# Fifth block product of Q in a two-level Winograd projection: quarter sums accumulated in PSUM onto ScalarE copies, interleaved with the seventh block product

## The chip, the cores and the metric

The kernel runs on one core of a Trainium2 chip. The metric is device time in microseconds (us) of the whole program; lower is better. TensorE (PE in the profile) multiplies, with its weight loads listed apart as PEld; VectorE is DVE, ScalarE is ACT, GpSimd is POOL, and SyncE (SP) issues the transfers.

## The reference

Two layers of the same form are applied to `x` of shape (8, 512, 32, 32), all in float32. Cut to what matters here, one layer is

```python
xn = group_norm(x) * gn_scale + gn_bias              # per image; xt is (512 channels, 1024 positions)
qkv = einsum('oc,bcn->bon', qkv_w, xt) + qkv_b       # three 512x512 weights times 512x1024
q, k, v = split(qkv, 3)                              # 8 heads of 64
attn = softmax(einsum('bhdi,bhdj->bhij', q, k) / 8)
out = einsum('bhij,bhdj->bhdi', attn, v)
out = einsum('oc,bcn->bon', proj_w, out) + proj_b + x
```

Eight images and two layers make 16 units, worked one after the other.

## The kernel before, in words

**Order of a unit.** A unit first forms Q, then K, then V (the first unit: Q, V, K), then the output projection of the unit before it, and then runs attention over 64 steps. Everything is issued in an order written out by hand, on in-order engine queues; callbacks `done(g)` place DVE and POOL work of other kinds between the products. A recording layer adds the semaphore waits. PSUM is held in four tiles of two banks (128 x 2 x 512 float32): `sbank[0]` and `sbank[1]`, which appear as `s` in the profile, and `apair[0]` and `apair[1]`, which appear as `a`.

**Block products.** Each projection splits its operands 2 by 2 and forms seven block products (Winograd's form of Strassen's scheme) in `blocks` (L422), with P1 to P7 combined into four output blocks: C11 = P1 + P2, and with U2 = P1 + P6 and U3 = U2 + P7, C22 = U3 + P5, C21 = U3 + P4, C12 = U2 + P5 + P3. A plain block product for Q and K, `block_product` (L405), is four matmul calls of 128 x 512, two for each of two row halves; each call is two PE matmuls. The tile of products 1 and 2 is `bx` = `apair[0]`; of 6, 7 and 4 it is `by` = `sbank[0]`; of 5 and 3 it is `bz` = `apair[1]`. The order is 1, 6, 2, 7, 5, 4, 3. After 6, `summed` forms u2 from `by` on DVE; after 7 it forms u3 (two operations at L624), and product 4 then accumulates onto what 6 and 7 left in `by`.

**Inner products.** In 15 of the 16 units (all but the first) some block products are formed by seven quarter products of 128 x 256 again: 2, 5, 4 and 3 of Q; 1, 2, 7, 5, 4 and 3 of K; 2, 3 and 4 of the output projection. `inner_products` (L437) runs the quarter products in the order `ORDER` = 1, 2, 3, 6, 5, 4, 7 (for Q). Quarters 2, 3 and 4 go straight into three quarters of the block's own tile. Quarters 1, 6 and 7 are accumulated one after the other in one place, `one`, and 5 in another, `two`; after each of these four ACT copies that place to a fresh SBUF tile `rest` (L460), so that `rest` holds 1, 1+6, 1+6+7 and 5. POOL then adds two quarters of `rest` to others (`fold`, L466 to L469) and adds `rest` to the result (`rests`, L650, or L647 and L648 where a half has to be split). For Q's product 2, `one` is in `sbank[1]` and `two` in `apair[1]`; for its product 5, `one` is in `sbank[1]` and `two` in `apair[0]`; for 4, `apair[0]` and `sbank[1]`.

**What follows.** `c11` (L605) evacuates C11 of Q by two ACT operations between product 2 and product 7. `others` (L636, L637) forms C22, C21 and C12 on DVE. The right factors of the inner products come from four subtractions each: those of 2 and 5 on POOL before the unit starts (L1088), those of 4 and 3 on POOL in between (L578), those of K's 1 and 7 on DVE in between (L578 too). K's P1 is summed on DVE at L492 to L495 from `bx` and `rest`.

Of the kernel before, what the change touches and what calls it, by code (L numbers as in the profile page):

```python
# [18 lines left out]
P = 128  # L19
# [13 lines left out]
def fast_path(ctx, tc, x, qkv_wT, proj_wT, vecs, groups, out, flag):  # L33
# [15 lines left out]
    nc = tc.nc  # L49
# [4 lines left out]
    FD = 512  # L54
    NH = N // FD
    H = P // 2
    FD2 = FD // 2
# [6 lines left out]
    def pool(name, bufs, **kw):  # L64
        return ctx.enter_context(tc.tile_pool(name=name, bufs=bufs, **kw))
# [9 lines left out]
    tpool = pool("tpool", 1)  # L75
    tmppool = pool("tmppool", 1)
    trpool = pool("trpool", 2)
# [7 lines left out]
    sbank = [ps.tile([P, 2, FD], F32, tag=f"s{i}", name=f"s{i}") for i in range(2)]  # L85
# [316 lines left out]
    class Unit:  # L402
        pass

    def block_product(bank, a, b, tokens, start, stop, between=None):  # L405
        for i in range(4 if tokens else 2):
            if i == 1 and between is not None:
                between()
            if tokens:
                dst = bank[:, i // 2, (i % 2) * FD2 : (i % 2 + 1) * FD2]  # L410
            else:
                dst = bank[:, i, :]
            for c in range(2):
                at, moving = (b, a) if tokens else (a, b)

                nc.tensor.matmul(  # L416
                    dst, at[:, c, ts(i, P)], moving[:, c, :],
                    start=start and c == 0 and not (tokens and i % 2),
                    stop=stop and c == 1, skip_group_check=True,
                )  # L420

    def blocks(name, left, right, tokens, c11, others, done, u3_in, summed, inner={}, rests=None,  # L422
               u2_in=(trpool, "tr"), between=None, behind=None, p1=None):

        bx, by, bz = apair[0], sbank[0], apair[1]
        sums, taken = [], []

        def products(bank, k, start, stop, between=None):
            block_product(bank, left[k], right[k], tokens, start, stop, between)

        def inner_products(bank, k, first=False):  # L437

            if k not in inner:
                products(bank, k, first, k != 5)
                return None
            a, b, one, two, order, room = inner[k]
            one, two, rest = one[:, 0, :FD2], two[:, 0, :FD2], room(f"m{k}_{name}")
            dst = {
                1: one, 6: one, 7: one, 5: two,
                2: bank[:, 0, :FD2], 3: bank[:, 0, FD2:], 4: bank[:, 1, :FD2],
            }
            to = {  # L450
                1: rest[:, 0, :FD2], 6: rest[:, 0, FD2:], 7: rest[:, 1, :FD2], 5: rest[:, 1, FD2:]
            }

            def step(j):
                nc.tensor.matmul(  # L455
                    dst[j], a[j], b[j], start=j in (1, 5) or first and j in (2, 4),
                    stop=j not in (1, 6), skip_group_check=True,
                )
                if j in to:
                    taken.append(nc.scalar.copy(to[j], dst[j]))  # L460

            for j in order if k != 1 else order[:-1]:
                step(j)
            return (rest, partial(step, order[-1])) if k == 1 else rest

        def fold(rest):  # L466
            add = nc.gpsimd.tensor_add
            add(rest[:, 0, FD2:], rest[:, 0, FD2:], rest[:, 1, FD2:])  # L468
            add(rest[:, 1, FD2:], rest[:, 1, :FD2], rest[:, 1, FD2:])  # L469

        def add_rest(r, h, rest, alone=None):

            if rest is not None:
                fold(rest)
                rests(r, h, rest, alone)

        def work(pool, tag, k):
            sums.append(pool.tile([P, 2, FD], F32, tag=tag, name=f"{k}_{name}"))
            return sums[-1]

        fresh = p1 is not None or 1 in inner
        if p1 is not None:
            sums.append(p1)
            done(sums)
            products(by, 6, True, False)
        elif fresh:
            p1 = work(accpool, "acc", "p1")
            rest, last = inner_products(bx, 1, True)
            done(sums)
            products(by, 6, True, False, last)  # L490
            add = nc.vector.tensor_add
            add(rest[:, 0, FD2:], rest[:, 0, FD2:], rest[:, 1, FD2:])  # L492
            add(p1[:, 0, :], bx[:, 0, :], rest[:, 0, :])
            add(p1[:, 1, :FD2], bx[:, 1, :FD2], rest[:, 1, :FD2])
            add(p1[:, 1, FD2:], rest[:, 1, :FD2], rest[:, 1, FD2:])  # L495
        else:
            products(bx, 1, True, False, between)
            if behind is not None:
                behind()
            p1 = work(accpool, "acc", "p1")  # L500
            nc.scalar.copy(p1, bx)  # L501
            done(sums)
            products(by, 6, True, False)
        u2 = work(*u2_in, "u2")
        summed(0, u2, by, p1)
        done(sums)
        rest = inner_products(bx, 2, fresh)
        c11(bx, p1 if fresh else None, rest)
        add_rest(0, 0, rest)
        done(sums)  # L510
        seventh = inner_products(by, 7)
        u3 = work(*u3_in, "u3")
        summed(1, u3, by, p1)
        if seventh is not None:
            fold(seventh)
        done(sums)
        twice = inner_products(bz, 5, True)
        others(1, 1, bz, u3, twice)
        add_rest(1, 1, twice, u3)
        if seventh is not None:  # L520
            rests(1, 1, seventh)
        done(sums)
        rest = inner_products(by, 4)
        others(1, 0, by, p1)
        add_rest(1, 0, rest)
        if seventh is not None:
            rests(1, 0, seventh)
        done(sums)
        rest = inner_products(bz, 3)
        others(0, 1, bz, u2, twice)  # L530
        add_rest(0, 1, rest, u2 if twice is not None else None)
        if twice is not None:
            rests(0, 1, twice)
        done(sums)
        return taken[-1:]

# [3 lines left out]
    ORDER, ORDER_5, ORDER_1 = (1, 2, 3, 6, 5, 4, 7), (1, 5, 2, 6, 3, 4, 7), (2, 3, 1, 4, 5, 6, 7)  # L540

    def room_of(pool, tag):
        return lambda name: pool.tile([P, 2, FD], F32, tag=tag, name=name)

    def inner_of(w, sel, left):


        x, z, s1 = apair[0], apair[1], sbank[1]
        p = room_of(ppool, "p")
        plan = {  # L550
            "q": {
                2: (s1, z, ORDER, room_of(tpool, "o1")), 5: (s1, x, ORDER, room_of(tpool, "o2")),
                4: (x, s1, ORDER, room_of(tpool, "o4")), 3: (s1, x, ORDER, room_of(tpool, "o1")),
            },
            "k": {
                1: (s1, z, ORDER_1, lambda _: w.k[1].rearrange("p (a b) -> p a b", a=2)),
                2: (s1, z, ORDER, room_of(tmppool, "tmp")), 7: (z, s1, ORDER, room_of(tpool, "o4")),
                5: (s1, x, ORDER_5, p), 4: (x, s1, ORDER, p), 3: (s1, x, ORDER, p),
            },
        }[sel]  # L560
        return {
            k: (inner_lefts(k, left[k], w.made[sel][k]), w.inner[k], *plan[k]) for k in INNER[sel]
        }

    def projections(w, rest, between=None):
# [4 lines left out]
        l, _ = units[u]  # L570
# [25 lines left out]
        def pairs(sel, bias):  # L596
            tiles = getattr(w, sel)
# [44 lines left out]
            def rests(r, h, rest, alone=None):  # L642
                add = nc.gpsimd.tensor_add
                for i in range(2):
# [4 lines left out]
                    else:  # L649
                        w.last[sel].append(add(cols, cols, rest[:, i, :]))  # L650

            left, inner = w.lefts["qk".index(sel)], {}
            if w.inner:
                inner = inner_of(w, sel, left)
            blocks(
                f"{sel}_{u}", left, w.right, False, c11, others, done,
                (accpool, "acc") if w.inner else (ppool, "p"), summed, inner, rests, **early[sel],
            )

        def values():  # L660
# [372 lines left out]
    tiles = [xn[:, c, :] for c in range(CC)]  # L1033
# [7 lines left out]
    right, mixing = mix_right("x_0", xn[:, :2], xn[:, 2:])  # L1041
# [10 lines left out]
    between, mixing_w = norm_first(xn, first_weights, mixing)  # L1052
# [14 lines left out]
    for u in range(2 * B):  # L1067
        w = Unit()
# [4 lines left out]
        for sel in "qk":  # L1073
            tiles = [
                qkpool.tile([P, N], F32, tag=sel, name=f"{sel}_{u}_{pr}") for pr in range(CC)
            ]
            setattr(w, sel, tiles)
        if u > 0:
            w.made, w.inner, parts = old.made_next, {}, {}
            for k in INNER["q"]:  # L1080
                room = ppool.tile([P, 4, FD2], F32, tag="p", name=f"r{k}_{u}")
                w.inner[k], parts[k] = mix_inner(right[k], room, nc.gpsimd)

            for k, pr in ((1, 3), (7, 2)):
                room = w.k[pr].rearrange("p (a b) -> p a b", a=4)
# [35 lines left out]
        between = None  # L1121
# [3 lines left out]
        if u + 1 < 2 * B:  # L1125
            xn = load_xn(u + 1)
            nxt = norm_parts(u + 1, xn)
            right, mixing = mix_right(f"x_{u + 1}", xn[:, :2], xn[:, 2:])
# [357 lines left out]
```

## Time and profile before

| what | value |
|---|---|
| median of three runs | 3257.72 us |
| the three runs | 3256.99, 3257.72, 3259.81 us |
| span of the profiled execution | 3256.9 us (first to last instruction; no other time of that execution is given) |
| PE busy, share of the span | 3244.5 us, 100% |
| DVE, ACT, POOL busy | 2715.3, 1650.2, 1216.3 us |
| granted TensorE clock, mean | 0.999 |
| PE matmuls of plain block products, 128 x 512 | one every 0.43 us |
| PE matmuls of inner products, 128 x 256 | one every 0.216 us |

Matmuls are pipelined: the duration shown for one (0.59 us for 512 columns, 0.38 us for 256) is longer than the spacing of two. The profile covers one execution; its span lies 0.8 us under the median.

### The profile page before, as it was taken

The page shows a single profiled execution, that of the slowest core. Times are in us where ns is not written, and L with a number is a line of the kernel's source. Part 1 is how long each engine was busy: PE and PEld are TensorE (multiplying, and loading weights), DVE is VectorE, ACT ScalarE, POOL GpSimd, SP SyncE. Part 2 cuts the span into 40 slices and gives each one's busy share as a digit, 9 for nine tenths or more (in the row PEclk, how much of TensorE's full clock was granted, in tenths as well). Part 3 has the DMA queues.
Part 4 walks back from the last instruction along what each step waited for, and adds up shares of the span by engine and source line. Part 5 has one row for each costly group of instructions (what it writes and reads, how often), then busy time and mean ns, then how long its engine had stood idle before and what let it go on. Part 6 is the DMA issues. An engine that isn't in the chain of part 4 may idle for free.

```text
span 3256.9 us, 56805 instructions
## 1 busy us (share of the span) xinstructions
PE 3244.5 (100%) x22206; PEld 1863.3 (57%) x22206; DVE 2715.3 (83%) x3488; ACT 1650.2 (51%) x2296; POOL 1216.3 (37%) x1207
## 2 busy tenths in 40 slices
PE   9999999999999999999999999999999999999999
PEld 5465474654746547465574655747556474564743
DVE  5887978789787897989979889797897978979786
ACT  1653626546274463744637446373563735637354
POOL 2054171531706317063270732607126071350710
PEclk9999999999999999999999999999999999999999
DMA  3112120121201212023120121201212012120111
GB/s 104 48 45 79 46 79 28 45 79 46 85 22 45 85 43 86 18 71 114 55 87 27 45 86 46 85 16 45 86 46 85 17 54 76 46 85 22 67 71 48
DMA packets 86463, 192.51 MB, mean 59 GB/s; under 512 B 22960, under 2 KB 34992, under 8 KB 84272
## 3 DMA queue, kind: packets, MB, share of 16 engines
q1 hardware_dynamic: 86192, 188.82, 17.0%
q8 instruction: 180, 2.95, 0.4%
q14 instruction: 91, 0.75, 0.1%
HBM read 148.00 MB, written 39.19 MB: 57 GB/s over the span
## 4 chain that ended last, share of the span: by engine, by line
PE 96%; DVE 3%; issue 0%; DMA 0%; ACT 0%; SPq 0%; DVEq 0%
PE a L848 26%; PE s L820 25%; PE s L416 14%; PE a L416 12%; PE a L455 10%; PE s L455 9%; DVE acc L867 1%; PE a L820 1%; PE s L766 0%; PE a L766 0%; DVE tr L880 0%; PE s L361 0%; DVE acc L865 0%; DVE ao L874 0%; DMA xn<-x_dram 0%
## 5 line engine op out<-in xcount | busy, mean ns | idle before, releaser
L828 ACT ACTIVATE p<-s 128x1024 f32<-128x1024 f32 x976 | 998.0, 1024 | 558.0 <-PE s L820 516.6
L848 PE MATMUL a<-p,v 64*64 64x512 f32 x8192 | 1099.8, 589 | 0.0
L820 PE MATMUL s<-q,k 64*64 64x512 f32 x7808 | 1058.1, 590 | 0.0
L867 DVE TENSOR_TENSOR acc<-acc,p 128x1024 f32<-128x1024 f32 x768 | 968.6, 1261 | 61.7 <-ACT p L828 13.0
L848 PEld LDWEIGHTS a<-p,v 64*64 64x64 f32 x8192 | 383.2, 131 | 495.8 <-ACT p L828 350.2
L820 PEld LDWEIGHTS s<-q,k 64*64 64x64 f32 x7808 | 383.5, 133 | 431.9 <-issue 422.8
L1088 POOL TENSOR_TENSOR r<-xn 128x256 f32<-128x256 f32 x30 | 49.5, 1649 | 1175.7 <-DVE acc L867 1038.3
L650 POOL TENSOR_TENSOR k<-k,m_k 128x512 f32<-128x512 f32 x180 | 259.6, 1463 | 0.0
L865 DVE TENSOR_TENSOR acc<-p,p 128x1024 f32<-128x1024 f32 x128 | 156.2, 1220 | 20.5 <-ACT p L828 13.9
L312 POOL TENSOR_TENSOR y<-var,half 128x4 f32<-128x4 f32 (+1 forms) x17 | 33.2, 1950 | 344.4 <-DVE var L310 344.4
L880 DVE STREAM_TRANSPOSE tr<-acc 128x1024 f32<-128x1024 f32 x128 | 157.9, 1234 | 0.0
L650 POOL TENSOR_TENSOR q<-q,m_q 128x512 f32<-128x512 f32 x120 | 157.2, 1325 | 0.0
L890 DVE TENSOR_REDUCE red<-tr 128x32 f32<-128x1024 f32 x128 | 154.4, 1206 | 0.6
L538 DVE TENSOR_TENSOR u_v<-s,p_v 128x1024 f32<-128x1024 f32 x32 | 39.2, 1224 | 123.7 <-PE s L416 123.7
L501 ACT COPY p_o<-a 128x1024 f32<-128x1024 f32 x15 | 15.2, 1012 | 244.2 <-PE a L416 244.2
L874 DVE TENSOR_TENSOR ao<-a,tmp 128x512 f32<-128x512 f32 x128 | 88.0, 688 | 60.9 <-ACT tmp L873 59.6
L460 ACT COPY m_q<-s 128x256 f32<-128x256 f32 x150 | 55.9, 373 | 145.3 <-PE s L455 142.7
L468 POOL TENSOR_TENSOR m_o<-m_o 128x256 f32<-128x256 f32 x45 | 34.2, 760 | 251.7 <-ACT m_o L460 251.7
L416 PE MATMUL s<-x_t,s2w 128*128 128x512 f32 x256 | 117.5, 592 | 0.0
L416 PE MATMUL a<-w,xn 128*128 128x256 f32 x496 | 112.1, 379 | 0.0
L460 ACT COPY m_k<-s 128x256 f32<-128x256 f32 x165 | 61.5, 373 | 93.8 <-PE s L455 90.2
L334 ACT ACTIVATE xn<-xn,shift,scale 128x512 f32<-128x512 f32 x124 | 99.5, 804 | 10.9 <-DVE shift L330 10.9
(291 smaller groups left out, 5130.5 us busy)
## 6 DMA issues: line engine op xcount, KB each, us to landing
rb<-drec SPq DMA_DIRECT2D x128, 256.0 KB, 3.9
xn<-mid SPq DMA_DIRECT2D x36, 512.0 KB, 7.9
il<-ilk SPq DMA_DIRECT2D x15, 1152.0 KB, 7.0
xn<-x_dram SPq DMA_DIRECT2D x32, 512.0 KB, 7.0
x<-x_dram SPq DMA_DIRECT2D x32, 512.0 KB, 5.5
x<-mid SPq DMA_DIRECT2D x28, 512.0 KB, 4.9
il<-ilq SPq DMA_DIRECT2D x15, 768.0 KB, 4.2
mid<-u_o SPq DMA_DIRECT2D x32, 256.0 KB, 2.1
```

Source lines behind the costliest of these rows:

```text
L334: nc.scalar.activation(cols, cols, AF.Identity, bias=st["shift"][:, c - lo : c - lo + 1], scale=st["scale"][:, c - lo : c - lo + 1],)
L416: nc.tensor.matmul(dst, at[:, c, ts(i, P)], moving[:, c, :], start=start and c == 0 and not (tokens and i % 2), stop=stop and c == 1, skip ...
L455: nc.tensor.matmul(dst[j], a[j], b[j], start=j in (1, 5) or first and j in (2, 4), stop=j not in (1, 6), skip_group_check=True,)
L460: taken.append(nc.scalar.copy(to[j], dst[j]))
L650: w.last[sel].append(add(cols, cols, rest[:, i, :]))
L820: nc.tensor.matmul(bank[e * H : (e + 1) * H, j, :], w.k[pr][j * H : (j + 1) * H, t * P + e * H : t * P + (e + 1) * H], w.q[pr][j * H : (j ...
L828: exp = nc.scalar.activation(p, bank, AF.Exp, scale=SCALE)
L848: nc.tensor.matmul(banks[r][j * H : (j + 1) * H, :], w.v[rows, t, lo : lo + D], p[rows, j, :], start=(t == 0), stop=(t == NT - 1),)
L865: nc.vector.tensor_add(acc, state["first"], p)
L867: nc.vector.tensor_add(acc, acc, p)
L880: nc.vector.transpose(tr, state["acc"].pop(c))
L890: nc.vector.tensor_reduce(red[:, :, qh, :], state["tr"].rearrange("p j (f i) -> p j f i", i=BL), AX.X, ALU.add)
```

## The change

The change concerns Q's fifth block product in the 15 units with inner products. Its quarter sums are no longer all copied to SBUF. A new function `seeded` runs the quarters in the order 1, 6, 7, 5, 2, 3, 4. Quarter 1 is formed in `one`, and ACT copies it into the first quarter of `bz`; quarter 6 is accumulated onto it, and ACT copies 1+6 into the third quarter of `bz`; quarter 7 goes to `two`, and ACT copies it to an SBUF tile `late`; quarter 5 is accumulated onto 1+6, and ACT copies that into the second and the fourth quarter of `bz`. Quarters 2, 3 and 4 are then accumulated onto the copies. `one` and `two` are the two banks of `sbank[1]`. The four matmul calls of the seventh block product (a 0 in the sequence below) are issued in between, as `fillers`. `lates` adds `late` on POOL, by one operation for each of two output blocks. The second place of Q's product 2 moves from `apair[1]` to the second bank of `sbank[1]`. `fold` and `rests` of the fifth product are no longer called.

```diff
@@ block_product @@
+                step = partial(
+                    nc.tensor.matmul, dst, at[:, c, ts(i, P)], moving[:, c, :],
...
+                if steps is None:
+                    step()
+                else:
+                    steps.append(step)
@@ blocks @@
+        def seeded(bank, k, fillers, scratch, room):
+            a, b = inner[k][:2]
+            one, two = scratch[:, 0, :FD2], scratch[:, 1, :FD2]
+            late = room(f"m{k}_{name}")[:, 0, :FD2]
+            dst = {
+                1: one, 6: one, 5: one, 7: two,
+                2: bank[:, 0, :FD2], 3: bank[:, 0, FD2:], 4: bank[:, 1, :FD2],
+            }
+            seeds = {
+                1: [bank[:, 0, :FD2]], 6: [bank[:, 1, :FD2]], 5: [bank[:, 0, FD2:], bank[:, 1, FD2:]],
+                7: [late],
+            }
+            fillers = iter(fillers)
+            for j in (1, 0, 6, 7, 0, 5, 2, 0, 3, 0, 4):
+                if j == 0:
+                    next(fillers)()
+                    continue
+                nc.tensor.matmul(
+                    dst[j], a[j], b[j], start=j in (1, 7), stop=j not in (1, 6), skip_group_check=True
+                )
+                for to in seeds.get(j, ()):
+                    taken.append(nc.scalar.copy(to, dst[j]))
+            return late
...
-        seventh = inner_products(by, 7)
+        late, seventh = None, None
+        if seed is not None:
+            steps = []
+            block_product(by, left[7], right[7], tokens, False, True, steps=steps)
+            late = seeded(bz, 5, steps, *seed)
+        else:
+            seventh = inner_products(by, 7)
         u3 = work(*u3_in, "u3")
         summed(1, u3, by, p1)
...
-        twice = inner_products(bz, 5, True)
+        if late is not None:
+            twice = None
+        else:
+            twice = inner_products(bz, 5, True)
         others(1, 1, bz, u3, twice)
+        if late is not None:
+            lates(1, 1, late)
...
+        if late is not None:
+            lates(0, 1, late)
@@ inner_of @@
-                2: (s1, z, ORDER, room_of(tpool, "o1")), 5: (s1, x, ORDER, room_of(tpool, "o2")),
+                2: (s1, s1[:, 1:, :], ORDER, room_of(tpool, "o1")), 5: (s1, x, ORDER, room_of(tpool, "o2")),
@@ pairs @@
+            def lates(r, h, late):
+                cols = tiles[2 * r + 1][:, ts(h, FD)].rearrange("p (a b) -> p a b", a=2)
+                w.last[sel].append(
+                    nc.gpsimd.tensor_add(cols, cols, late[:, None, :].to_broadcast([P, 2, FD2]))
+                )
...
+                if sel == "q":
+                    seed = sbank[1], room_of(tpool, "o2")
```

More of the change, by code (lines that the diff above doesn't have):

```diff
@@ L403, in fast_path, with block_product @@
         pass
-    def block_product(bank, a, b, tokens, start, stop, between=None):
+    def block_product(bank, a, b, tokens, start, stop, between=None, steps=None):
         for i in range(4 if tokens else 2):
@@ L414, in block_product @@
                 at, moving = (b, a) if tokens else (a, b)
-                nc.tensor.matmul(
-                    dst, at[:, c, ts(i, P)], moving[:, c, :],
+                step = partial(
+                    nc.tensor.matmul, dst, at[:, c, ts(i, P)], moving[:, c, :],
                     start=start and c == 0 and not (tokens and i % 2),
@@ L420, in block_product @@
                 )
+                if steps is None:
+                    step()
+                else:
+                    steps.append(step)
     def blocks(name, left, right, tokens, c11, others, done, u3_in, summed, inner={}, rests=None,
-               u2_in=(trpool, "tr"), between=None, behind=None, p1=None):
+               u2_in=(trpool, "tr"), between=None, behind=None, p1=None, seed=None, lates=None):
         bx, by, bz = apair[0], sbank[0], apair[1]
@@ L650, in rests @@
                         w.last[sel].append(add(cols, cols, rest[:, i, :]))
+            def lates(r, h, late):
[3 more added lines that the diff above has]
+                )
             left, inner = w.lefts["qk".index(sel)], {}
+            seed = None
             if w.inner:
                 inner = inner_of(w, sel, left)
+                if sel == "q":
+                    seed = sbank[1], room_of(tpool, "o2")
             blocks(
@@ L657, in pairs @@
                 (accpool, "acc") if w.inner else (ppool, "p"), summed, inner, rests, **early[sel],
+                seed=seed, lates=lates,
             )
```

## Prediction

> **What bounds the kernel.** I read the busy shares first, then the chain that ended last:
>
> ```profile
> PE 3244.5 (100%) x22206; PEld 1863.3 (57%) x22206; DVE 2715.3 (83%) x3488; ACT 1650.2 (51%) x2296; POOL 1216.3 (37%) x1207
> PE 96%; DVE 3%; issue 0%; DMA 0%; ACT 0%; SPq 0%; DVEq 0%
> ```
>
> PE is the chain from end to end. A busy share alone could hide slow spacing, so next came PE's timeline in the unit whose Q starts at about 1004 us; positions below are us after 1010.51, where block product 2 begins.
>
> ```profile
> 1012.66 0.59 PE L455 MATMUL a<-r,w 128*128 128x256 f32 x2
> 1013.10 0.59 PE L455 MATMUL s<-r,w 128*128 128x256 f32 x2
> 1013.53 3.60 PE L416 MATMUL s<-xn,w 128*128 128x512 f32 x8
> 1016.96 0.59 PE L455 MATMUL s<-x_t,s1w 128*128 128x256 f32 x2
> ...
> 1019.55 0.59 PE L455 MATMUL s<-r,s1w 128*128 128x256 f32 x2
> ```
>
> A quarter product starts every 0.43 us and a call of the seventh block product every 0.86, without a pause. The waits of the weight loads name only two small ones here, once in each of 15 units:
>
> ```profile
> PEld a L455 <- ACT m_k L460: 3.6, 15, 0.2
> PEld a L455 <- POOL r L578: 3.5, 15, 0.3
> ```
>
> At each the matmul lasts 0.48 instead of 0.38 us, so each costs some 0.11. Any pause that the change puts on PE lengthens the kernel by itself; work taken off POOL or DVE can return at most such a wait.
>
> [...] The built program of the change is stricter: its list of waits guards each two-bank tile as a whole. The trace of before agrees in so far as, in Q, a quarter on the tile of a copied one never stands less than two steps behind it. [...] the clock is 0.999 before. [...] DVE's `k<-xn` of 128x256 beside POOL averages 1.10 us, `ro<-ao` of that size 0.65.
>
> **The price of a PE wait.** Quarter 6 of the fifth product starts at 1018.26, its second matmul ends at 1018.85, and its copy starts 0.04 later:
>
> ```profile
> 1013.73 0.37 ACT L460 COPY m_q<-s 128x256 f32<-128x256 f32 x1 [0.49 <-PE s L455]
> 1014.00 1.27 ACT L605 ACTIVATE q<-a,vec 128x512 f32<-128x512 f32 x2
> ...
> 1018.89 0.37 ACT L460 COPY m_q<-s 128x256 f32<-128x256 f32 x1 [0.92 <-PE s L455]
> ```
>
> So a copy ends 1.00 us after its quarter starts (0.63 + 0.37). The return to PE is shown once at full length, in a later unit:
>
> ```profile
> 1618.65 1.22 DVE L179 TENSOR_TENSOR xn<-xn 128x1024 f32<-128x1024 f32 x1
> ...
> 1619.92 0.30 PEld L416 LDWEIGHTS s<-xn,w 128*128 128x128 f32 x2 [1.03 <-DVE xn L179]
> 1619.92 1.13 PE L416 MATMUL s<-xn,w 128*128 128x512 f32 x2 [0.63 <-DVE xn L179]
> ```
>
> DVE ends at 1619.87, the weight load starts 0.05 later, and the first matmul runs 0.105 longer than usual: PE is back 0.16 after the release. A quarter that must wait for the copy of an earlier one therefore can't start sooner than **1.16 us** behind it. Directly behind (0.43) it stalls 0.73; with one quarter between (0.86) 0.30; with a filler or two quarters between, nothing.
>
> **The change part by part.** PE's matmuls stay as many (13,155 in both programs). The waits in the changed program's order of instructions give, for one unit:
>
> 1. Product 2 has `two` in the same tile as `one`. Quarter 5, directly behind 6, waits for 6's copy: +0.73. Quarter 7 waits for 5's copy with only 4 between: +0.30. It then starts at 3.62.
> 2. The fifth product's quarter 1 now follows that 7 directly and waits for its copy; before, the seventh's 3.43 us lay between. +0.73; it starts at 4.78.
> 3. Its copy queues on ACT behind `c11` (1.27 us, now about 4.52 to 5.79), ends near 6.06, and quarter 6, due at 6.07 behind a filler, waits: +0.15 (0 to 0.25).
> 4. Quarter 7 writes the other bank of the tile, directly behind 6: +0.73. Quarter 5 waits for 7's copy behind a filler: 0.
> 5. Quarter 2, directly behind 5, waits for both of 5's copies into `bz`, and the second waits for the first: 0.63 + 0.37 + 0.05 + 0.37 + 0.16 = 1.58, less 0.43: +1.15. Quarters 3 and 4 follow freely.
> 6. u3 waits for the last filler. Before, DVE ran it under the fifth product:
>
> ```profile
> 1017.16 1.41 DVE L624 SCALAR_TENSOR_TENSOR u_q<-s,vec,p_q 128x512 f32<-128x512 f32 x2
> 1019.75 1.02 DVE L636 TENSOR_TENSOR q<-a,u_q 128x512 f32<-128x512 f32 x2 [1.18 <-PE a L455]
> ```
>
> Now only quarter 4 of the fifth and quarter 1 of product 4 follow. The filler ends at 13.00, u3 at 14.45, PE is back at 14.61; quarter 2 of product 4, which waits for both u3 operations, was due at 13.70: +0.90.
>
> 7. Queued behind u3 on DVE are C22, K's factors, C21, C12 and K's P1. C22 and C12 add 512 instead of 256 columns in one half: +0.26 each. From the end of C22 (1020.77) to the end of L494 DVE is nearly gapless, and PE is just behind it:
>
> ```profile
> 1032.33 0.41 DVE L494 TENSOR_TENSOR p_k<-a,k 128x256 f32<-128x256 f32 x1
> 1032.80 0.41 PEld L455 LDWEIGHTS a<-xn,w 128*128 128x128 f32 x2
> ```
>
> C22 will end 5.5 us later (at 15.73), L494 then 5.7, PE by the steps so far 4.6. K's product 2 waits for the difference, about 1.0, less what a less crowded POOL gives back: I take +0.70 (0 to 1.0).
>
> 8. POOL loses 9 and gains 3 operations in a unit, some 5.7 us less. Only the wait on `r` L578 goes, because PE comes later: -0.11. Otherwise POOL's slack is not PE's: its last K add ends at 1069.4, and the scores that need it start at 1094.9. The two late adds (about 1.3 each) hide there too. ACT's fifth copy is counted in 5. No transfer is moved, and SP's queue is untouched.
>
> Sum: 0.73 + 0.30 + 0.73 + 0.15 + 0.73 + 1.15 + 0.90 = 4.69; + 0.70 - 0.11 = **5.28 us per unit**, 79.2 us in 15. Against the profiled execution, 3256.9 + 79.2 = 3336.1; the median lies 0.8 over that span, so **3337 us** (+2.4%).
>
> **Unknown prices.** A ScalarE copy into PSUM could take 0.30 us ([...] the size is my estimate from 0.37 less a fifth) or 0.47; four lie on the path: -0.28 to +0.40. u3 could start 0.1 earlier. With steps 3 and 7 at their ends this gives 4.05 to 6.08 per unit: 3319 to 3349.
>
> **Rivals.** (a) The clock falls: stalls fill about a third of 14 us in each unit. If one 3.4 us window ran at half clock, that adds 1.7 us per unit: 3362. Against it: no single pause reaches 1.2 us. (b) The waits don't bite, the one on the other side: if PE and ACT hand over inside the 0.43 us to the next quarter, nothing stalls, and POOL's 0.11 per unit is gained: about 3256. It decides where the added wait per unit falls under 0.43 us (0.2%, about what a measurement of this kernel can tell from no change, is 6.5 us, over 15). Against it stands the measured round trip of 1.16. (c) DVE catches up, because POOL's thinner load shortens K's factor subtractions, and copies into PSUM are short: 4.05 per unit, 3319.
>
> **Numbers.** Main sum, with the bounds above, 0.82; (c) and below 0.08; (a) 0.06; (b) 0.04, split into 0.03 within 0.2% and 0.01 faster. The range is 3319 to 3349, widened by the 2.8 us that the three runs differ by: 3316 to 3352.
>
> **What would show it.** In the new profile, waits of PE's weight loads for ACT copies in Q, six or seven per unit, near 0.7 us each and 1.2 before the fifth's quarter 2; one for DVE's u3 of 0.9; one in K's product 2 for DVE's sum of K's P1; none on `r`. PE busy time hardly up, with idle time of some 80 us. POOL some 85 us less busy. It is wrong if quarter 7 of the fifth starts 0.43 behind 6, or if PE's clock leaves 1.00.

## The result, and the profile after

The changed kernel takes **3348.64 us** (median of 4 runs, 3347.55 to 3349.89) against 3258.01 for the kernel before (4 runs, 3256.99 to 3259.81): ratio **1.0276**, 95% interval 1.0263 to 1.0290. That is 90.6 us more; forecast were 79. The time lies in the stated range, 3316 to 3352, close to its upper end. The profiled execution took 3348.1 us, its span 3346.3, at a mean PE clock of 1.000.

The busy line and the chain that ended last, from the page of after:

```profile
PE 3273.2 (98%) x22206; PEld 1856.7 (55%) x22206; DVE 2698.4 (81%) x3488; ACT 1652.7 (49%) x2311; POOL 1127.3 (34%) x1117
PE 96%; DVE 2%; ACT 1%; issue 0%; DMA 0%; POOL 0%; DVEq 0%; POOLq 0%
```

PE has as many instructions as before. It has 73.1 us of idle time instead of 12.4, and ACT, 0% of the chain before, is now in it. POOL is 89 us less busy, and none of that shows in the time. PE's busy time itself rose by 28.7 us. That isn't more work: back to back, the records of two quarter products overlap (each lasts 0.59 us, one starts every 0.43); a pause takes the overlap away, and the waiting matmul's record is longer (0.70). So a pause is booked partly as idle and partly as busy time, and has to be measured between ends.

Which waits these are, the waits view of after for PE tells (line that waits, what it waited for and the line of that: us in total, times, longest):

```profile
PE a L458 <- DVE p_k L523: 16.5, 15, 1.1
PE a L488 <- ACT a L492: 12.5, 15, 0.8
PE s L458 <- DVE u_q L666: 9.6, 15, 0.6
PE s L488 <- ACT a L492: 7.5, 14, 0.5
PE s L458 <- ACT m_q L463: 6.9, 15, 0.5
PE s L488 <- ACT m_q L463: 6.9, 15, 0.5
```

L458 is the line of the usual quarters and L463 that of their copies on ACT; L488 is the line of `seeded`'s quarters and L492 that of their copies; L666 is u3, L523 the sum of K's P1 (L494 before). Each wait comes once in each of 15 units; the one listed 14 times is put down to POOL's `r` (L620) in the remaining unit. Four have an ACT copy as their releaser and two have DVE. In the kernel before, the same view has none of them.

The prediction also expected no wait on `r`. The small one before, of a weight load in Q's product 3, is gone. The waits of the weight loads in after do name POOL's `r` (L620) for `seeded`'s quarters 6 and 7, 30 times, 25.3 us in all. The stalls at these places are still the copies': in the unit below an ACT copy ended after that `r`, and quarter 7's stall goes when only its bank is moved, with POOL's list unchanged (experiment on step 4).

Four pairs from PE's timeline of after, in the unit that the prediction followed (start, duration, in brackets the idle time before and its releaser):

```profile
1040.37 0.67 PE L488 MATMUL s<-r,il 128*128 128x256 f32 x2
1041.58 0.67 PE L488 MATMUL s<-r,s1w 128*128 128x256 f32 x2 [0.54 <-ACT a L492]
...
1042.95 0.59 PE L488 MATMUL s<-r,il 128*128 128x256 f32 x2
1044.38 0.70 PE L488 MATMUL a<-x_t,s1w 128*128 128x256 f32 x2 [0.83 <-ACT a L492]
...
1047.49 0.59 PE L458 MATMUL a<-x_t,w 128*128 128x256 f32 x2
1048.72 0.70 PE L458 MATMUL s<-x_t,w 128*128 128x256 f32 x2 [0.64 <-DVE u_q L666]
...
1060.90 0.59 PE L458 MATMUL s<-xn,w 128*128 128x256 f32 x2
1062.59 0.70 PE L458 MATMUL a<-xn,w 128*128 128x256 f32 x2 [1.09 <-DVE p_k L523]
```

From end to end the last pair is 1063.29 - 1061.49 = 1.80 us apart, where two quarters in step are 0.43 apart: a stall of 1.37. In the same way the others give 0.78 (the fifth's quarter 7 behind 6), 1.11 (quarter 2 behind 5) and 0.91 (product 4's quarter 2, on u3). All of them by the prediction's steps, as the mean over the units:

| step | stall | forecast us | measured us |
|---|---|---|---|
| 1 | product 2's quarters 5 and 7 | 0.73 + 0.30 | 0.73 + 0.30 |
| 2 | the fifth's quarter 1 | 0.73 | 0.73 |
| 3 | quarter 6, its copy behind `c11` | 0.15 | 0.21 |
| 4 | quarters 7 and 5 | 0.73 + 0 | 0.78 + 0 |
| 5 | quarter 2, behind two copies | 1.15 | 1.10 |
| 6 | product 4's quarter 2, on u3 | 0.90 | 0.91 |
| 7 | K's product 2, on K's P1 | 0.70 | **1.37** |
| 8 | the wait on `r` that goes | -0.11 | -0.11 |
| | sum of a unit | 5.28 | 6.02 |

15 times 6.02 is 90.3 us, the whole of the 90.6. One term is out of size, step 7. The experiments ask whether each stall really has the cause that the sum gives it, and why step 7 is twice its forecast.

### The profile page after: what moved, and what is told of

The parts are those of the page before. It is cut to its first block, busy times and chain, and to the rows that moved or that the text cites. A ratio compares the mean times of both kernels' runs of the same rounds, so it can differ in the third digit from the quotient of the medians.

```text
span 3346.3 us, 56773 instructions
## 1 busy us (share of the span) xinstructions
PE 3273.2 (98%) x22206; PEld 1856.7 (55%) x22206; DVE 2698.4 (81%) x3488; ACT 1652.7 (49%) x2311; POOL 1127.3 (34%) x1117
## 4 chain that ended last, share of the span: by engine, by line
PE 96%; DVE 2%; ACT 1%; issue 0%; DMA 0%; POOL 0%; DVEq 0%; POOLq 0%
PE a L900 26%; PE s L872 25%; PE a L421 12%; PE s L421 12%; PE a L458 8%; PE s L458 8%; PE s L486 2%; PE a L872 1%; PE s L488 1%; DVE u_q L666 1%; PE a L488 1%; ACT a L492 0%; PE s L818 0%; PE a L818 0%; DVE acc L919 0%
## 5 line engine op out<-in xcount | busy, mean ns | idle before, releaser
L666 DVE SCALAR_TENSOR_TENSOR u_q<-s,vec,p_q 128x512 f32<-128x512 f32 x64 | 45.1, 746 | 116.6 <-PE s L486 97.1
L692 POOL TENSOR_TENSOR q<-q,m_q 128x512 f32<-128x512 f32 x90 | 117.5, 1326 | 15.4 <-DVE q L679 15.4
L463 ACT COPY m_k<-s 128x256 f32<-128x256 f32 x165 | 61.4, 372 | 114.3 <-PE s L458 110.8
```

## The experiments

Each is an edit of the changed kernel, but for one that edits the kernel before. Times are medians. The kernel before took 3259.0 to 3259.3 us beside them, about 1 us more than in the result above, and the changed kernel was not run again; a difference to it is therefore good to about 1 us.

**Product 2's quarters apart (step 1).** The second place goes back to `apair[1]`.

```diff
-                2: (s1, s1[:, 1:, :], ORDER, room_of(tpool, "o1")), 5: ...
+                2: (s1, z[:, 1:, :], ORDER, room_of(tpool, "o1")), 5: ...
```

> Changed kernel, with the second place of Q's product 2 in the second bank of apair[1] instead of the second bank of sbank[1]. Theory (PE waits for copies of its own PSUM tile): the pauses before quarters 5 and 7 of product 2 (0.73 and 0.30 us) go, nothing else moves: 1.03 us in 15 units, -15.5 us, 3333 us. Rival (the time is ScalarE's own work, five copies instead of four and two writes more into PSUM): nothing of that is changed, 3348 us.

Measured: 3332.5 us (ratio 1.0227, 1.0210 to 1.0244), 16.1 under the changed kernel; 15 x 1.03 is 15.5. The two stalls are gone, and no other moved.

**The same part alone, in the kernel before.**

```diff
-                2: (s1, z, ORDER, room_of(tpool, "o1")), 5: ...
+                2: (s1, s1[:, 1:, :], ORDER, room_of(tpool, "o1")), 5: ...
```

> Kernel before, with only one thing of the change: the second place of Q's product 2 moved into the second bank of sbank[1]. Theory: +0.73 and +0.30 us per unit, less the 0.11 us wait on POOL's r that PE then no longer reaches: +0.92 in 15 units, +13.8 us, 3272 us. Rival (the time comes with the seeded product alone): 3258 us.

Measured: 3273.7 us (ratio 1.0046, 1.0029 to 1.0063), 14.7 over the kernel before. The waits view of this kernel has one new wait that comes in every unit:

```profile
PE s L455 <- ACT m_q L460: 6.9, 15, 0.5
```

It is the 6.9 us that after shows at its L458: quarter 5's stall of 0.73, of which the view books 0.46 as idle. Quarter 7's 0.30 is too short to leave idle time in the records and shows only between ends. Both stalls have the size that they have in after, and the wait on `r` is gone here too: 15 times 1.03 - 0.11 is 13.8. So this part costs the same without the fifth product's change, and the terms of the sum can be added.

**The fifth's quarter 7 in a bank of its own (step 4).**

```diff
-            one, two = scratch[:, 0, :FD2], scratch[:, 1, :FD2]
+            one, two = scratch[:, 0, :FD2], bx[:, 0, :FD2]
```

> Changed kernel, with quarter 7 of the fifth product in apair[0] instead of the second bank of sbank[1]. Theory: the pause before quarter 7 (0.78 us in the trace of after) goes, quarter 5 then stands 1.29 us behind 6 and needs 1.16, so no new one comes: -11.6 us, 3337 us. Rival (ScalarE's own work): as many copies of the same size, 3348 us.

Measured: 3337.1 us (ratio 1.0239, 1.0222 to 1.0256), 11.6 under the changed kernel, or 0.77 a unit. Quarter 7 doesn't wait once its bank lies in another tile, though it follows quarter 6 as closely as before. What it waited for was the copy of quarter 6, which reads another bank of the same tile. This is the guard by the tile as a whole, and not by the bank, that the prediction read off the built program.

**K's seventh factor on POOL (step 7).** DVE's queue between C22 and K's P1 loses four of its eight subtractions `k<-xn`; POOL takes them up behind Q's C21.

```diff
-    w.inner[k], parts[k] = mix_inner(right[k], room, nc.vector)
+    w.inner[k], parts[k] = mix_inner(right[k], room, nc.vector if k == 1 else nc.gpsimd)
...
-    ((2, 4), (3, 3), (5, 1), (7, 7))
+    ((2, 4), (3, 3), (5, 1), (6, 7))
```

> Changed kernel, with the four subtractions for K's product 7 on POOL, behind Q's C21, instead of on DVE, behind Q's C12. Theory (the 1.37 us before K's product 2 is DVE's queue, which u3 started late): DVE reaches K's P1 some 4 us earlier and the wait goes: -20.5 us, 3328 us. Rival (that wait comes from the copies or from PE's own products): 3348 us, or above, since POOL's factors could come late for K's product 7.

Measured: 3328.5 us (ratio 1.0215, 1.0198 to 1.0232), 20.1 under the changed kernel; 15 x 1.37 is 20.6. K's wait is gone and every other stall stands. So K's product 2 waited for DVE's queue, and the 1.37 is all of what that queue costs.

**Q's rests left out (why step 7 is 1.37).** The kernel leaves out POOL's additions of `rests` for Q, so its Q is incomplete; DVE's instructions stay as they are.

```diff
-                for i in range(2):
+                for i in range(2 if sel == "k" else 0):
                     cols = tiles[2 * r + i][:, ts(h, FD)]
```

> Changed kernel, without the POOL additions of rest to Q's result for products 2, 4 and 3 (left out of the computation: six operations of 512 columns in each of 15 units). Theory 1 (DVE's operations collide with POOL's longer ones, which added 0.44 us to DVE's chain where 0.3 of relief was forecast): DVE's chain from C22 to K's P1 falls from 12.67 to 11 us or less, the wait before K's product 2 from 1.37 to some 0 to 0.4: -15 to -20 us, 3328 to 3334 us. Theory 2 (the chain is long by DVE's own queue and its wider operations): the chain stays within 0.3 us, 3344 to 3348 us.

Measured: 3328.0 us (ratio 1.0213, 1.0196 to 1.0230). K's wait is gone here too, with DVE's list of operations unchanged. From the end of C22 to the end of K's P1 DVE takes 11.95 us before, 12.67 after and 10.34 here. The timelines of after, for DVE and then POOL, show the end of that stretch (start, duration):

```profile
1058.52 1.48 DVE L620 TENSOR_TENSOR k<-xn,k 128x256 f32<-128x256 f32 x1
1059.92 1.48 DVE L521 TENSOR_TENSOR k<-k 128x256 f32<-128x256 f32 x1
...
1058.28 2.85 POOL L692 TENSOR_TENSOR q<-q,m_q 128x512 f32<-128x512 f32 x2
```

In the kernel before, the same two places:

```profile
1030.64 0.94 DVE L492 TENSOR_TENSOR k<-k 128x256 f32<-128x256 f32 x1
...
1031.27 2.94 POOL L650 TENSOR_TENSOR q<-q,m_q 128x512 f32<-128x512 f32 x2
```

And DVE with Q's rests left out:

```profile
1054.16 0.41 DVE L521 TENSOR_TENSOR k<-k 128x256 f32<-128x256 f32 x1
```

The last 256-column operations into `k` take 0.41 us each here; in before and after such an operation takes 0.83 to 0.95 where POOL runs 256-column operations throughout, and up to 1.48 beside its 512-column additions. Not every DVE operation gets longer: in before, the two 256-column sums into `p_k` (L494 and L495) run wholly beside that pair and take 0.41. Before, POOL reached its pair of 512-column additions (2.94 us) only when DVE's last subtraction was two thirds done. After the change POOL has less to do, so it comes to that pair ahead of DVE's last two subtractions, and both take 1.48. The prediction had DVE's `k<-xn` beside POOL at a mean of 1.10 us; what it missed is the timing. The experiment shows that POOL's additions make DVE's stretch long; that the change made it longer by their earlier start is read from the timelines, as no run moved that pair alone.

**The seventh's products all ahead of the fifth's.**

```diff
-            for j in (1, 0, 6, 7, 0, 5, 2, 0, 3, 0, 4):
+            for j in (0, 0, 0, 0, 1, 6, 7, 5, 2, 3, 4):
```

> Changed kernel, with all four calls of the seventh product ahead of the fifth's quarters (1, 6, 7, 5, 2, 3, 4 then follow directly). Theory: product 2 keeps 1.03 us; quarters 6, 7, 5 and 2 wait 0.73, 0.78, 0.73 and 1.10; u3 again runs under the fifth product, so its 0.91 goes, and DVE's queue is no longer late by it, so of the 1.37 before K's product 2 some 0.6 stays (DVE's wider operation and its collisions with POOL): 4.86 us per unit with the 0.11 gained, 3331 us. Rival (the wait in K is POOL's collisions alone, whatever u3 does): 1.37 stays, 3342 us. Rival (the fillers are what keeps the change from costing more): above 3349 us.

Measured: 3355.5 us (ratio 1.0295, 1.0277 to 1.0312), a miss; the time is that of the last rival. u3's stall is gone as expected, and K's wait is not: 1.45 in undisturbed units. C22 then waits for PE's quarter 4 instead of for u3, and DVE's stretch behind it again has a mean of 12.67 us. With the stalls of this order (1.03 in product 2, 0.78, 0.78, 0.73 and 1.10 at quarters 6, 7, 5 and 2, 1.45 in K, less 0.11: 5.76 a unit) the time should be 3345. The rest is PE's clock: 0.993 in the mean (0.993 to 0.996 in all four runs), at half speed in ten of the 15 units, for one stretch of 3.41 us or two. The windows view shows the stretch ahead of one and that stretch (from:to, length, then busy us (instructions) of PE, PEld, DVE, ACT, POOL, then PE clock, DMA share, GB/s), and below them a stretch in another unit, whose clock did not fall:

```profile
1047.20:1050.60 3.40, 1.60 (x5) 0.83 (x6) 0.00 (x0) 1.44 (x4) 3.32 (x5) 1.00 0.34 78
1050.60:1054.00 3.40, 3.40 (x9) 2.65 (x9) 0.79 (x2) 0.00 (x0) 1.23 (x2) 0.50 0.00 0
...
1463.60:1467.00 3.40, 1.99 (x7) 1.16 (x8) 0.00 (x0) 1.09 (x3) 3.32 (x5) 1.00 0.34 76
```

No stall in `seeded`, ahead of these stretches, is over 1.10 us. The starts of the slow stretches lie whole multiples of 3.4133 us apart (422.529, 634.155 and 842.368 us: 62 and 61 of them), so it looks like a fixed grid; in the trace of before the clock stands at 1.00 for 3242.662 us, 950 times that length. Set on that grid, every stretch in this run's 15 units with 1.90 us or less of recorded PE work was followed by a slow one, and none with 1.99 or more, but for two that were slow themselves. The border need not hold elsewhere: at the start of the program, in the run with quarter 7 in a bank of its own, a stretch with 1.65 us (from 7.57 to 10.98 us) was not followed by a slow one. But for those two, recorded work filled 46 to 56% of the stretches ahead of a slow one (1.58 to 1.90 us); none was idle. At half speed a quarter starts every 0.85 us instead of 0.43 (1051.21, 1052.06 and 1052.91 us), so a stretch full of work loses half its length, and the 41 us in slow stretches could cost 20 at most. Some 11 are left in the time: in six units DVE catches up in the meantime, with K's wait down to between 0.34 and 0.52, and not every slow stretch is full of work.

**The same order with quarter 7 apart (is it the share of work?).** The edits of the two experiments on the order and on quarter 7, together.

> The fillers-first order with quarter 7 of the fifth product moved to the free bank of bx. Theory 1, the TensorE clock answers to the idle share of a fixed stretch of 3.41 us: with fillers first the worst such stretch had 75% idle in every unit and the clock halved behind stretches of 62% and more; the kernel with the change as made has 52% at most and kept its clock. Here quarter 7's 0.73 is gone and quarter 5 stalls 0.30 instead of 0.78, so the fifth product's pauses are 0.78 + 0.30 + 1.10, at most 63% of a stretch where the stretch happens to lie right: none to two low windows. Stalls of a unit 0.73 + 0.30 + 0.78 + 0.30 + 1.10, K's wait 1.45, less 0.11: 4.55, in 15 units 68 us: 3327 (3323 to 3331). Theory 2, the clock falls because the seventh's fillers no longer lie between the fifth's pauses, however long these are: some ten low windows again, +10 us: 3337. K's wait should stay at 1.45, since C22 still stands directly before the chain on DVE.

Measured: 3325.7 us (ratio 1.0207, 1.0190 to 1.0224). No slow stretch came in any unit. The emptiest stretch on the grid has this line in the windows view of this run:

```profile
2480.60:2484.00 3.40, 2.01 (x8) 0.99 (x7) 1.22 (x2) 1.80 (x5) 3.34 (x4) 1.00 0.62 157
```

Its 2.01 us of work lie just above the 1.99 that kept the clock in the other run. The seventh's products are as far from the fifth's pauses as there, so their place by itself isn't the cause; less idle time in a stretch was enough to keep the clock. Nor did it hang on where the grid happened to lie: no stretch of that length in these units, wherever it is laid, has less than 2.01 us. K's wait is 1.45 again, as expected.

**All cures together.** Quarters of product 2 apart, quarter 7 in `bx`, K's seventh factor on POOL, and a filler behind each quarter that is waited for:

```diff
-            for j in (1, 0, 6, 7, 0, 5, 2, 0, 3, 0, 4):
+            for j in (0, 1, 0, 6, 7, 0, 5, 0, 2, 3, 4):
```

> The seeded product with its waits spread out: product 2's second place in apair[1], quarter 7 in apair[0], the order seventh-1-seventh-6-7-seventh-5-seventh-2-3-4, and K's product 7's subtractions on POOL. Theory: of the waits only 0.24 us before quarter 2 and up to 0.15 us on u3 remain: 3261 to 3265 us, within 0.2 per cent of before; nothing is gained, since PE did not wait before. Rival (seeding in PSUM itself costs, by ScalarE's copies): 3290 us or more. Rival (POOL's shorter list returns time): below 3252 us.

Measured over 20 runs: 3264.05 us (ratio **1.0016**, 1.0009 to 1.0023). Its busy line:

```profile
PE 3249.7 (100%) x22206; PEld 1863.0 (57%) x22206; DVE 2677.0 (82%) x3428; ACT 1652.6 (51%) x2311; POOL 1177.1 (36%) x1177
```

The stalls left are 0.24 at quarter 2, 0.08 at quarter 6, and 0.17 in K's product 7, where the kernel before already has 0.11. PE is at 100% again and the time is that of before and a little more (4.8 us). POOL has 39 us less to do than before, and this brings nothing, since PE never waited for POOL but for the 0.11. So the change in this version costs nearly nothing and brings nothing, and no version that was run beats the kernel before.

## Why the prediction was right, and where it was off

**The price and steps 1, 2, 4 and 5 held.** A quarter that waits for the copy of the one directly before it stalls 0.73 to 0.78 us, with one quarter between 0.30, with a filler between 0. Taking away step 1 or step 4 by itself returned its own sum, and step 1 put alone into the kernel before cost its own sum, less the wait on `r`. Steps 2 and 5 have no run of their own; with all cures together, a filler between took step 2's stall away and brought step 5's from 1.10 to 0.24. The rival in which the waits don't bite is out.

**Copies into PSUM** were an unknown price. The source view of L492 in after gives them, and beside them the one copy of the same line into SBUF (times in ns: least, median, most):

```profile
L492 ACT COPY a<-s x60: 357/357/394, 209.2 to 3120.9; 128x256 f32<-128x256 f32 x60
L492 ACT COPY m_q<-s x15: 372/372/372, 211.7 to 3119.2; 128x256 f32<-128x256 f32 x15
```

They are 15 ns shorter, 4%, far from the fifth of the prediction's estimate. Quarter 2 passes two of them, and its 1.10 against 1.15 has room for that. Quarter 7 stalls 0.05 more than the price, and the source view of L488 shows what goes with it (the same columns; PEldq is the queue of the weight loads):

```profile
L488 PEldq EVENT_SEMAPHORE  x30: 51/51/51, 209.7 to 3118.4; - x30
```

These 30 stand ahead of the weight loads of quarters 6 and 7, once each in a unit. From the end of the copy to the weight load of quarter 7 it is 0.11 us instead of 0.05, which with the copy 0.015 shorter gives the 0.05. With all fillers first, quarters 6 and 7 have this record and stall 0.78; quarter 5 has none and stalls 0.73. The copy's target alone doesn't make the difference: with fillers first and quarter 7 apart, quarter 5 waits for a copy into PSUM without such a record, one quarter between, and stalls 0.28. No run took the record away, so it is not shown to be the cause.

**Step 3** came out at 0.21, inside its bounds, and **step 6** at 0.91 for 0.90: u3 became late as soon as the last filler did, and its cure (fillers first) took exactly this stall away.

**Step 7 is the term that was mis-sized**: 1.37 for 0.70. The prediction had the difference between C22's delay and PE's at about 1.0 and took off 0.3, "less what a less crowded POOL gives back". C22's end came where it was forecast, at 15.70 us for 15.73. Behind it DVE's stretch had 0.26 of wider C12 less the 0.3 of relief, as the step has it; measured, it grew by 0.72 (11.95 to 12.67). By parts, from the timelines: the first four subtractions -0.26, C21 and C12 +0.11, the last four +0.36, the final `k<-k` +0.54, the two sums behind it -0.03. So the relief came in the first group, and over three times as much was lost again at the end, where POOL's 512-column additions now lie beside the last subtractions. That is 0.76 more than the step had; C22 came 0.03 earlier and PE 0.07 later than forecast, which leaves the 0.67. Without POOL's additions for Q's rests the same DVE operations take 2.33 us less (12.67 to 10.34) and the wait is gone. 0.67 x 15 is 10 of the 11.6 us between forecast and result.

That the total still fell inside the range is in part luck. The 1.37 lies outside the bounds that the step gave itself (0 to 1.0), and the measured 3348.6 is just under the main sum's upper bound, 3349: the allowance for dearer copies into PSUM, 0.40 a unit, was not needed and made room for it.

The rival in which DVE catches up had the sign of this effect wrong: POOL's thinner load didn't shorten DVE's stretch (11.95 us before, 12.67 after), as POOL arrived earlier, at a worse moment.

**Step 8** held: POOL lost 89 us for 85, and only the wait on `r` paid for it.

**The clock rival** did not come in the changed kernel (1.000). What it reckoned with, 3.4 us at half clock, is what the fillers-first order showed: 3.41 us at 0.50. The reason given against it, that no single pause reaches 1.2 us, is too weak: in the fillers-first order no stall ahead of a slow stretch was over 1.10 us, and the clock fell. By that run's border what kept it here was the sum over a stretch: the emptiest 3.4 us in after's 15 units have 2.03 us of recorded PE work. The rival was nearer than the forecast had it.

**"PE busy time hardly up"** was off as a reading of the page: busy time took 28.7 us of the stalls, idle time 60.7.

## What to carry to other kernels

Where PE is the bound, a sum formed in PSUM on top of a copy turns a DVE or POOL addition into a round trip PE, ACT, PE, here 1.16 us from one quarter's start to that of the one that waits; it was free only where at least that much independent work of PE lay between the two, and two outputs in one tile waited for each other's readers even though they don't share data (0.77 us a unit here). Work taken off an engine that nobody waited for brought nothing here, and made that engine early elsewhere (DVE's last `k<-k` took 1.48 us beside it instead of 0.94): look at what its next long operations then lie beside. Price the queue behind the waiting instruction operation by operation with the neighbours that it will have, not with a mean from the trace of before.

## What the runs showed of the hardware that was not expected

- In the 15 units of one run, PE's clock went to half for stretches of 3.413 us on a fixed grid after stretches with 1.58 to 1.90 us of recorded work (no stall in them over 1.10 us), and stayed up after 1.99 and more. In the changed kernel and in the fillers-first order with quarter 7 apart, no stretch of the units has less than 2.01 us, and the clock stayed up.
- ScalarE's copy of 128x256 f32 at L492 took 357 ns into PSUM and 372 into SBUF (medians in after).
- DVE's 128x256 operations into `k` took 0.41 us with Q's rests left out, 0.83 to 0.95 beside POOL's 256-column operations and up to 1.48 beside its 512-column additions; its sums into `p_k` took 0.41 beside the latter.
- A quarter waiting for the copy of the one directly before it stalled 0.73 us, or 0.78 where an `EVENT_SEMAPHORE` record of 51 ns stood ahead of its weight load.
